# The shift of 32 layer norms computed on GpSimd instead of VectorE, in a Mamba block with a dense mixture of experts

## The chip, the cores and the metric

The kernel runs on one core of a Trainium2 chip. The metric is the device time of one execution in microseconds; lower is better. The core's engines each work through a queue of their own in order and wait for each other by semaphores: TensorE (PE in the profile; its weight loads are PEld), VectorE (DVE), ScalarE (ACT), GpSimd (POOL) and SyncE (SP, which only issues DMAs here).

## The reference

The input x has 16 sequences of 256 tokens, each token 128 numbers. All is float32. Cut to what matters:

```python
def block(x):                                    # the Mamba block
    x = x + mamba(layernorm(x, ln1_g, ln1_b))    # norm "a"
    h = layernorm(x, ln2_g, ln2_b)               # norm "b"
    return x + relu(h @ ffn_w1.T + ffn_b1) @ ffn_w2.T + ffn_b2

def experts(x):                                  # all 8 experts for every token
    return sum((silu(x @ Wg[e]) * (x @ Wu[e])) @ Wd[e] for e in range(8))

x = layernorm(x + block(x))                      # norm "c"
x = layernorm(x + experts(x))                    # norm "e"

# inside mamba, for each of 256 channels and 16 states, along the 256 tokens:
h = exp(dt * A) * h + dt * B * xc
y = sum over states of h * C;  y = (y + D * xc) * silu(z)
```

A layer norm is (x - mean) / sqrt(variance + 1e-5) over the 128 numbers of a token. Written as x * rs + nb, rs is the variance plus 1e-5 to the power -1/2, and nb = -mean * rs is the shift that this case is about.

## The kernel before, in words

The 4096 tokens go through in eight groups of 512. The tokens of a group lie on the 128 partitions in four columns of tokens, so each norm of a group has four means and four powers per partition: tiles of 128x4. Eight groups times the four norms a, b, c, e make 32 norms.

The work of a group is cut into stages, written as Python generators: `stage_a` (norm a, projections, convolution, and `dt`, ending with `u` = dt * xc on GpSimd, L369), the scan over 32 pairs of channel half and state, `stage_c` (output projection `po` L504, norm b, the two-layer network `pf` L549 and `pff` L539, norm c), the experts (`pg` L596, `pu` L605, `acc` L615, with the SiLU on ScalarE at L598 and the product on VectorE at L606), and `stage_e` (norm e and the store). The scan does four things for each of its 32 steps: the decay `dA` on ScalarE (L441), the injection `dBx` on GpSimd (L452), the recurrence and the product `hC` on VectorE (L460, L462), and the sum into `y`, which is on TensorE (L479) while there are no experts to run and on GpSimd (L481) otherwise. `yt` (L489, VectorE) multiplies the finished y by the gate, and `po` reads it.

The order of all instructions is written out by hand in strings of one-letter words: `PRE` before the first scan, `FILL` until the first group reaches its experts, `TURN` after that. A word advances one thing: `s` a scan step, `i` an injection, `d` a decay, `a` an addition into y, `u`, `x`, `w` the three parts of an expert slice, `m` a filler of four transposes on TensorE (L715), and a capital letter moves every running stage of a kind on to its next `yield`. So the place of a stage's instruction in its engine's queue is set by the number of `yield`s ahead of it, and each queue is then worked through in this order. The experts of one group run among the scan of the next.

A norm is in three parts. `norm_stats` takes statistics on VectorE (L244, L246), adds 1e-5 (`ve`, L248), and raises to -1/2 on GpSimd (`rs`, L250). Two `yield`s later `norm_shift` makes the shift on VectorE in one instruction (`nb`, L256: mean times -1 times rs). `norm_apply` then makes four instructions on ScalarE with rs as scale and nb as bias (L262). In `stage_c` two additions on GpSimd make the second residual: `res` = x1 + x (L516), issued right after the power of norm b, and `res` + bias (L520), issued after the shift.

Of the kernel before, what the change touches and what calls it, by code (L numbers as in the profile page):

```python
# [8 lines left out]
FP = mybir.dt.float32  # L9
AF = mybir.ActivationFunctionType  # L10
ALU = mybir.AluOpType

P = 128
# [8 lines left out]
NTT = TB // P  # L22
# [82 lines left out]
def kernel(  # L105
# [25 lines left out]
    nc = tc.nc  # L131
# [11 lines left out]
    small = ctx.enter_context(tc.tile_pool(name="small", bufs=4))  # L143
# [91 lines left out]
    def as4(t):  # L235
        return t.rearrange("p (c d) -> p c d", d=DM)

    def norm_stats(src, name):

        n = src.shape[1]  # L240
        st = small.tile([P, NTT, 6], FP, tag="st", name=f"st_{name}")
        mv = small.tile([P, NTT, 2], FP, tag="mv", name=f"mv_{name}")
        for c in range(n):
            nc.vector.bn_stats(st[:, c, :], src[:, c, :])  # L244
        for c in range(n):
            nc.vector.bn_aggr(mv[:, c, :], st[:, c, :])  # L246
        ve = small.tile([P, NTT], FP, tag="ve", name=f"ve_{name}")
        nc.vector.tensor_scalar(ve[:, :n], mv[:, :n, 1], EPS, None, ALU.add)  # L248
        rs = small.tile([P, NTT], FP, tag="rs", name=f"rs_{name}")
        nc.gpsimd.tensor_tensor(rs[:, :n], ve[:, :n], mhalf[:, :n], ALU.pow)  # L250
        return mv[:, :n, 0], rs[:, :n]

    def norm_shift(stats, name):
        mean, rs = stats
        nb = small.tile([P, NTT], FP, tag="nb", name=f"nb_{name}")[:, : mean.shape[1]]
        nc.vector.scalar_tensor_tensor(nb, mean, -1.0, rs, ALU.mult, ALU.mult)  # L256
        return rs, nb

    def norm_apply(src, dst, scale):
        rs, nb = scale  # L260
# [49 lines left out]
    def stage_a(g):  # L310
        xt = x_tiles[g]
        s = state[g] = {}
        yield
        stats = norm_stats(xt, f"a{g}")
        yield
        yield
        scale = norm_shift(stats, f"a{g}")
        yield
        xh = wide("xh", f"xh{g}", 2, W[g])
        norm_apply(xt, as4(xh), scale)  # L320
        yield
        pt = yield from take(f"pxn{g}", W[g])
        transpose(pt, as4(xh))
        yield
        xn = wide("xn", f"xn{g}", 2, W[g])
        nc.scalar.activation(xn, pt, AF.Identity, bias=b1_sb[:, 0:1], scale=g1_sb[:, 0:1])
        done(f"pxn{g}")
        yield
        s["conv"] = set()
        s["xc"] = wides("xc", f"xc{g}", 2, NH, W[g])  # L330
        for h in range(NH):
            conv = stage_conv(g, h, xn)
            next(conv)
            next(conv)
            running["B" if g == 1 else "A"].append(conv)
        if g < 2:
            running["G"].append(stage_gate(g, xn))
        while (NH - 1) not in s["conv"] or 0 not in s["conv"]:
            yield
            yield  # L340
        R = DTR + 2 * NS
        pd = yield from take(f"pd{g}", W[g])
        for h in range(NH):
            nc.tensor.matmul(
                pd[0:R, :], lhsT=xpw[:, h, :], rhs=s["xc"][:, h, :], start=(h == 0), stop=(h == NH - 1)
            )
        yield
        dbc = act.tile([R, TB], FP, tag="dbc", bufs=2, name=f"dbc{g}")[:, : W[g]]
        nc.scalar.copy(dbc, pd[0:R, :])  # L349
        done(f"pd{g}")  # L350
        bc = s["bc"] = dram.tile([2 * NS, TB], FP, tag="bc", name=f"bc{g}")[:, : W[g]]
        nc.scalar.dma_start(out=bc, in_=dbc[DTR:R, :])
        yield
        dt = s["dt"] = wides("dt", f"dt{g}", 2, NH, W[g])
        u = s["u"] = wides("u", f"u{g}", 2, NH, W[g])
        for h in range(NH):
            pv = yield from take(f"pv{g}_{h}", W[g])
            nc.tensor.matmul(pv, lhsT=dtw[:, bass.ts(h, P)], rhs=dbc[0:DTR, :], start=True, stop=True)
            yield
            nc.scalar.activation(dt[:, h, :], pv, AF.Identity, bias=dtb[:, h : h + 1])  # L360
            done(f"pv{g}_{h}")
            yield
        yield from silu_time()
        nc.scalar.activation(dt, dt, AF.Softplus)  # L364
        yield
        for h in range(NH):

            engine = nc.vector if g == 0 and h == 0 else nc.gpsimd
            engine.tensor_tensor(u[:, h, :], dt[:, h, :], s["xc"][:, h, :], ALU.mult)  # L369

            engine.memset(dt[:, h, :].rearrange("p (b l) -> p b l", l=L)[:, :, 0:1], FAR)
            if g > 0:
                yield
                yield
        s["ready"] = True
        if g > 1:
            yield from stage_gate(g, xn)
# [118 lines left out]
    def stage_c(g):  # L496
        s = state[g]
        xt = x_tiles[g]
        xtf = xt.rearrange("p c d -> p (c d)")
        yield  # L500
        po = yield from take(f"po{g}", W[g])
        for c in range(W[g] // P):
            for h in range(NH):
                nc.tensor.matmul(  # L504
                    po[:, bass.ts(c, P)], lhsT=s["yt"][:, h, bass.ts(c, P)], rhs=outw[:, h, :],
                    start=(h == 0), stop=(h == NH - 1),
                )
        yield
        yield
        x1 = wide("x1", f"x1{g}", 1, W[g])  # L510
        nc.vector.tensor_add(x1, po, xtf)
        done(f"po{g}")
        stats = norm_stats(as4(x1), f"b{g}")

        res = wide("res", f"res{g}", 1, W[g])
        nc.gpsimd.tensor_tensor(res, x1, xtf, ALU.add)  # L516
        yield
        yield
        scale = norm_shift(stats, f"b{g}")
        nc.gpsimd.tensor_tensor(  # L520
            as4(res), as4(res), fb2_bc[:, :].unsqueeze(1).to_broadcast([P, W[g] // P, DM]), ALU.add
        )
        yield
        xh = wide("xh", f"x1h{g}", 2, W[g])
        norm_apply(as4(x1), as4(xh), scale)
        yield
        pt = yield from take(f"ph{g}", W[g])
        transpose(pt, as4(xh))
        yield
        h2 = wide("h2", f"h2{g}", 1, W[g])  # L530
        nc.scalar.activation(h2, pt, AF.Identity, bias=b2_sb[:, 0:1], scale=g2_sb[:, 0:1])
        done(f"ph{g}")
        yield
        r = wides("r", f"r{g}", 1, NF, W[g])
        po = None

        def second(f, start, stop):
            for c in range(W[g] // P):
                nc.tensor.matmul(  # L539
                    po[:, bass.ts(c, P)], lhsT=r[:, f, bass.ts(c, P)], rhs=w2[:, f, :],  # L540
                    start=start and c == 0, stop=stop and c == W[g] // P - 1, skip_group_check=True,
                )


        if g == 0:
            po = yield from take(f"pff{g}", W[g])
        for f in range(NF):
            pf = yield from take(f"pf{g}_{f}", W[g])
            nc.tensor.matmul(pf, lhsT=w1[:, bass.ts(f, P)], rhs=h2, start=True, stop=True)  # L549
            if g == 0 and f > 0:  # L550
                second(f - 1, f == 1, False)
            yield
            nc.scalar.activation(r[:, f, :], pf, AF.Relu, bias=fb1_sb[:, f : f + 1])  # L553
            done(f"pf{g}_{f}")
            yield
        if g > 0:
            po = yield from take(f"pff{g}", W[g])
            for f in range(NF - 1):
                second(f, f == 0, False)
                if f == 1:  # L560
                    yield
                    yield
        second(NF - 1, False, True)
        yield
        yield
        nc.vector.tensor_add(res, po, res)
        done(f"pff{g}")
        stats = norm_stats(as4(res), f"c{g}")
        yield
        yield  # L570
        scale = norm_shift(stats, f"c{g}")
        yield
        x2 = blocks("x2", f"x2{g}", 2, W[g] // P)
        norm_apply(as4(res), x2, scale)
        yield
        pt = yield from take(f"px{g}", W[g])
        transpose(pt, x2)
        yield
        x2T = wide("x2T", f"x2T{g}", 2, W[g])
        nc.scalar.copy(x2T, pt)  # L580
        done(f"px{g}")
        state[g] = dict(x2=x2, x2T=x2T)
        slices.extend((g, n) for n in range(NJ[g]))
        yield
# [35 lines left out]
    def stage_e(g):  # L620
# [8 lines left out]
        x2 = s["x2"]  # L629
        nc.vector.tensor_add(x2, as4(pt), x2)  # L630
        done(f"pao{g}")
        stats = norm_stats(x2, f"e{g}")
        yield
        yield
        scale = norm_shift(stats, f"e{g}")
        yield
        norm_apply(x2, x2, scale)
        nc.scalar.dma_start(out=tokens(out, g), in_=x2)
# [92 lines left out]
    while at["w"] < sum(NJ) or any(running.values()):  # L731
# [4 lines left out]
        g, k = scans[min(at["a"], len(scans) - 1)]  # L736
# [56 lines left out]
```

## Time and profile before

| | |
|---|---|
| median of 3 runs | 953.29 us (953.23 to 954.67) |
| the profiled execution's own time | 953.88 us |
| its span, first to last instruction | 952.1 us |
| TensorE busy | 909.8 us, 96% |
| VectorE busy | 755.6 us, 79% |
| ScalarE busy | 672.8 us, 71% |
| GpSimd busy | 662.4 us, 70% |
| mean granted clock of TensorE | 0.981 |

The page has one execution. Its slices show each engine's busy share in tenths over 40 equal pieces of the span, and the TensorE clock that was granted. A line of the timeline has the start in us from the first instruction, the length, engine, line of the kernel, operation, output and inputs, shape and count, and in brackets how long the engine stood idle before it and for whom. A line of the groups has the count, the busy time in us, the mean of one in ns, and the idle time before them in us with what ended it. A line of a table by stretch has the stretch in us, its length, and then for each engine its busy time and number of instructions, the granted clock, and the DMA share and rate.

A busy TensorE is not TensorE at its peak: ends of matrix products are modelled. Where a step of TensorE is measured here, it is from start to start.

### The profile page before, as it was taken

To read this page: it belongs to the slowest core of one execution; us is meant where nothing else is said; L and a number is where in the kernel's file an instruction comes from. 1 tells how busy PE (TensorE), PEld (TensorE's weight loads), DVE (VectorE), ACT (ScalarE), POOL (GpSimd) and SP (SyncE) were. 2 spreads that over 40 slices of the span, in tenths; PEclk is the share of its full clock that TensorE was granted. 3 is DMA by queue.
4 is the path that set the end of the run, shared out by engine and by line. 5 is a ranking of instruction groups with operands and counts; after the bars stand their busy time and mean duration, and the time that the engine had idled before them with its cause. 6 is when DMAs were issued, how large, how long until landed. Compare 5 with 4: busy or idle time off the path is not lost. (4 is left out here: it accounts for less than half of the span.)

```text
span 952.1 us, 9052 instructions
## 1 busy us (share of the span) xinstructions
PE 909.8 (96%) x2528; PEld 421.0 (44%) x2528; DVE 755.6 (79%) x1179; ACT 672.8 (71%) x965; POOL 662.4 (70%) x558
## 2 busy tenths in 40 slices
PE   8898889989999999999999999999999999999996
PEld 4344534445344543445344544454344544454442
DVE  4599897988889888997989888987989799723222
ACT  5833387769788788779787879879888877432121
POOL 1586486987699678988698869988698799500000
PEclk9799899999999999999999999999999999999998
DMA  7788764545356345446346354645445454000000
GB/s 202 259 294 279 242 220 158 182 143 186 124 180 224 126 155 168 179 142 219 116 149 226 111 176 154 210 131 197 144 154 176 150 196 174 1 0 12 0 1 11
DMA packets 56258, 146.88 MB, mean 154 GB/s; under 512 B 7688, under 2 KB 20880, under 8 KB 56208
## 3 DMA queue, kind: packets, MB, share of 16 engines
q1 hardware_dynamic: 51600, 143.69, 44.5%
q10 hardware_dynamic: 4608, 2.62, 1.0%
q8 instruction: 20, 0.33, 0.1%
q14 instruction: 30, 0.25, 0.1%
HBM read 143.67 MB, written 2.62 MB: 154 GB/s over the span
## 5 line engine op out<-in xcount | busy, mean ns | idle before, releaser
L460 DVE TENSOR_TENSOR_SCAN dA<-dA,dBx 128x512 f32<-128x512 f32 x256 | 312.8, 1222 | 26.4 <-ACT dA L441 24.0
L452 POOL TENSOR_TENSOR dBx<-B,u 128x512 f32<-128x512 f32 x256 | 321.1, 1277 | 11.3 <-DMA B<-bc 7.3
L481 POOL TENSOR_TENSOR y<-y,hC 128x512 f32<-128x512 f32 x217 | 277.5, 1281 | 11.4 <-DVE hC L462 5.5
L615 PE MATMUL acc<-h,wd 128*128 128x512 f32 x512 | 255.8, 599 | 0.0
L606 DVE TENSOR_TENSOR h<-pu,h 128x512 f32<-128x512 f32 x256 | 172.4, 684 | 101.2 <-PE pu L605 99.9
L596 PE MATMUL pg<-x2T,wg 128*128 128x512 f32 x512 | 251.7, 598 | 0.3 <-DVE h L606 0.2
L605 PE MATMUL pu<-x2T,wu 128*128 128x512 f32 x512 | 245.3, 594 | 0.9 <-ACT h L598 0.9
L598 ACT ACTIVATE h<-pg 128x512 f32<-128x512 f32 x256 | 146.3, 597 | 124.3 <-PE pg L596 122.6
L441 ACT ACTIVATE dA<-dt,A 128x512 f32<-128x512 f32 x256 | 170.3, 684 | 81.6 <-DVE hC L462 77.4
L462 DVE TENSOR_TENSOR hC<-dA,C 128x512 f32<-128x512 f32 x256 | 176.9, 691 | 14.4
L596 PEld LDWEIGHTS pg<-x2T,wg 128*128 128x128 f32 x512 | 96.8, 192 | 125.9 <-issue 103.6
L605 PEld LDWEIGHTS pu<-x2T,wu 128*128 128x128 f32 x512 | 96.3, 191 | 122.1 <-issue 98.7
L615 PEld LDWEIGHTS acc<-h,wd 128*128 128x128 f32 x512 | 94.6, 191 | 113.4 <-issue 110.6
L250 POOL TENSOR_TENSOR rs_e<-ve_e,mhalf 128x4 f32<-128x4 f32 x8 | 8.1, 1017 | 139.7 <-DVE ve_e L248 139.7
L598 ACT ACT_TABLE_LOAD x78 | 100.1, 1283 | 1.4
L441 ACT ACT_TABLE_LOAD x74 | 94.9, 1283 | 1.7 <-ACT dbc L349 0.4
L479 PE MATMUL py<-hC,ident 128*128 128x512 f32 x78 | 44.2, 674 | 7.9 <-DVE hC L462 7.9
L369 POOL TENSOR_TENSOR u<-dt,xc 128x512 f32<-128x512 f32 x15 | 19.6, 1305 | 33.0 <-ACT dt L364 33.0
L410 DVE SCALAR_TENSOR_TENSOR hc<-pi,cw,hc 128x510 f32<-128x510 f32 (+2 forms) x48 | 35.5, 745 | 5.3 <-ACT hc L403 4.1
L715 PE MATMUL busy<-ident 128*128 128x128 f32 x204 | 35.7, 302 | 2.8 <-POOL mhalf L191 1.4
L715 PEld LDWEIGHTS busy<-ident 128*128 128x128 f32 x204 | 25.9, 154 | 24.1 <-issue 10.5
L553 ACT ACTIVATE r<-pf,fb 128x512 f32<-128x512 f32 x32 | 21.2, 687 | 18.5 <-PE pf L549 18.5
(83 smaller groups left out, 592.8 us busy)
## 6 DMA issues: line engine op xcount, KB each, us to landing
B<-bc SPq DMA_DIRECT2D x128, 512.0 KB, 4.7
C<-bc SPq DMA_DIRECT2D x128, 512.0 KB, 4.7
xt<-in_x_dram SPq DMA_DIRECT2D x8, 256.0 KB, 4.3
wg<-in_Wg_dram SPq DMA_DIRECT2D x8, 256.0 KB, 6.0
wu<-in_Wu_dram SPq DMA_DIRECT2D x8, 256.0 KB, 5.7
wd<-in_Wd_dram SPq DMA_DIRECT2D x8, 256.0 KB, 6.1
out_dram<-x ACTq DMA_DIRECT2D x8, 256.0 KB, 5.0
bc<-dbc ACTq DMA_DIRECT2D x8, 64.0 KB, 1.6
```

Source lines behind the costliest of these rows:

```text
L441: nc.scalar.activation(s["dA", k], s["dt"][:, h, :], AF.Exp, scale=A_sb[:, h, n : n + 1])
L452: nc.gpsimd.tensor_tensor(s["dBx", k], s["B", k // NC][:, k % NC, :], s["u"][:, k // NS, :], ALU.mult)
L460: nc.vector.tensor_tensor_scan(dA, dA, s.pop(("dBx", k)), 0.0, ALU.mult, ALU.add)
L462: nc.vector.tensor_mul(hC, dA, s["C", k // NC][:, k % NC, :])
L479: nc.tensor.matmul(s["py"], lhsT=ident, rhs=hC, start=first, stop=False)
L481: nc.gpsimd.tensor_tensor(y, y, hC, ALU.add)
L596: nc.tensor.matmul(pg[:, cols], lhsT=wg[:, e, bass.ts(f, P)], rhs=s["x2T"], start=True, stop=True)
L598: nc.scalar.activation(s["h", j], pg, AF.Silu)
L605: nc.tensor.matmul(pu[:, cols], lhsT=wu[:, e, bass.ts(f, P)], rhs=s["x2T"], start=True, stop=True)
L606: nc.vector.tensor_mul(s["h", j], pu, s["h", j])
L615: nc.tensor.matmul(s["acc"], lhsT=wd[:, e, f, :], rhs=h[:, cols], start=(e == 0 and f == 0), stop=(e == NE - 1 and f == NF - 1),)
L715: nc.tensor.transpose(t[:, bass.ts(c, P)], ident, ident)
```

## The change

The shift is made inside `norm_stats`, right behind the power. VectorE now makes `nm`, minus the mean, ahead of `ve`. GpSimd multiplies it by rs (`nb`) directly after the power. `norm_shift` and its place two `yield`s later go away; the number of `yield`s up to `norm_apply` stays the same. In `stage_c` the first residual addition moves behind the two `yield`s, to the second.

```diff
         for c in range(n):
             nc.vector.bn_aggr(mv[:, c, :], st[:, c, :])
+
+        nm = small.tile([P, NTT], FP, tag="nm", name=f"nm_{name}")
+        nc.vector.tensor_scalar(nm[:, :n], mv[:, :n, 0], -1.0, None, ALU.mult)
         ve = small.tile([P, NTT], FP, tag="ve", name=f"ve_{name}")
         nc.vector.tensor_scalar(ve[:, :n], mv[:, :n, 1], EPS, None, ALU.add)
         rs = small.tile([P, NTT], FP, tag="rs", name=f"rs_{name}")
         nc.gpsimd.tensor_tensor(rs[:, :n], ve[:, :n], mhalf[:, :n], ALU.pow)
-        return mv[:, :n, 0], rs[:, :n]
-
-    def norm_shift(stats, name):
-        mean, rs = stats
-        nb = small.tile([P, NTT], FP, tag="nb", name=f"nb_{name}")[:, : mean.shape[1]]
-        nc.vector.scalar_tensor_tensor(nb, mean, -1.0, rs, ALU.mult, ALU.mult)
-        return rs, nb
+        nb = small.tile([P, NTT], FP, tag="nb", name=f"nb_{name}")
+        nc.gpsimd.tensor_tensor(nb[:, :n], nm[:, :n], rs[:, :n], ALU.mult)
+        return rs[:, :n], nb[:, :n]
...
     # stage_a; stage_c's norm c and stage_e alike
-        stats = norm_stats(xt, f"a{g}")
-        yield
-        yield
-        scale = norm_shift(stats, f"a{g}")
+        scale = norm_stats(xt, f"a{g}")
+        yield
+        yield
         yield
...
     # stage_c, norm b
-        stats = norm_stats(as4(x1), f"b{g}")
+        scale = norm_stats(as4(x1), f"b{g}")
+        yield
+        yield
 
         res = wide("res", f"res{g}", 1, W[g])
         nc.gpsimd.tensor_tensor(res, x1, xtf, ALU.add)
-        yield
-        yield
-        scale = norm_shift(stats, f"b{g}")
         nc.gpsimd.tensor_tensor(
             as4(res), as4(res), fb2_bc[:, :].unsqueeze(1).to_broadcast([P, W[g] // P, DM]), ALU.add
         )
```

More of the change, by code (lines that the diff above doesn't have):

```diff
@@ L567, in stage_c @@
         done(f"pff{g}")
-        stats = norm_stats(as4(res), f"c{g}")
+        scale = norm_stats(as4(res), f"c{g}")
         yield
         yield
-        scale = norm_shift(stats, f"c{g}")
         yield
@@ L631, in stage_e @@
         done(f"pao{g}")
-        stats = norm_stats(x2, f"e{g}")
+        scale = norm_stats(x2, f"e{g}")
         yield
         yield
-        scale = norm_shift(stats, f"e{g}")
         yield
```

## The prediction

> **What bounds the kernel now.** The page's slices come first: which engine is full, and where.
>
> ```profile
> PE   8898889989999999999999999999999999999996
> ...
> PEclk9799899999999999999999999999999999999998
> ...
> PE 14%; DVE 1%; issue 0%; ACT 0%; POOLq 0%; DVEq 0%
> ```
>
> A slice is 24 us. From the tenth slice on TensorE is full; the other engines have gaps. The last line is the chain that ended last: 14% of the span TensorE, nearly nothing else. In order of time that chain runs on TensorE without a gap from 805.71 to 942.36, and only the last norm follows. So norm work counts only where TensorE waits for it, and the next view is the timeline around TensorE's waits. Between 277 and 800 there is one large wait per group of tokens, at L504, and it comes back every 105.3 us. One such group, followed back:
>
> ```profile
> 569.80 1.02 POOL L250 TENSOR_TENSOR rs_e<-ve_e,mhalf 128x4 f32<-128x4 f32 x1 [7.71 <-DVE ve_e L248]
> 570.79 1.28 POOL L452 TENSOR_TENSOR dBx<-B,u 128x512 f32<-128x512 f32 x1
> ...
> 585.00 1.27 POOL L369 TENSOR_TENSOR u<-dt,xc 128x512 f32<-128x512 f32 x1 [0.50 <-ACT dt L364]
> ...
> 621.83 2.49 POOL L481 TENSOR_TENSOR y<-y,hC 128x512 f32<-128x512 f32 x2
> ...
> 623.14 1.73 DVE L489 TENSOR_TENSOR yt<-y,zg 128x512 f32<-128x512 f32 x1 [0.42 <-POOL y L481]
> ...
> 624.93 1.27 PE L504 MATMUL po<-outw,yt 128*128 128x128 f32 x9 [1.74 <-DVE yt L489]
> ```
>
> TensorE stands 1.74 us for yt; yt on VectorE stands 0.42 us for GpSimd's y; GpSimd has run without a pause since u at 585.00, and u waited 0.50 us for ScalarE's dt. So the period closes through TensorE, then dt on ScalarE, then u to y on GpSimd, yt, TensorE. The norms' GpSimd work (rs_b, rs_a, rs_c, rs_e) lies before u, never between u and yt. The five u of this kind (269, 374, 480, 585, 690) each have 0.50 to 0.52 us of slack. That slack is what the change must fit into.
>
> The other place is the start of the first expert work, where the engines wait for each other in turn:
>
> ```profile
> 104.25 0.17 DVE L248 TENSOR_SCALAR ve_b<-mv_b 128x4 f32<-128x4 f32 x1
> 104.50 1.01 POOL L250 TENSOR_TENSOR rs_b<-ve_b,mhalf 128x4 f32<-128x4 f32 x1 [7.95 <-DVE ve_b L248]
> 105.47 1.26 POOL L516 TENSOR_TENSOR res<-x,xt 128x512 f32<-128x512 f32 x1
> 105.54 1.21 DVE L256 SCALAR_TENSOR_TENSOR nb_b<-mv_b,rs_b 128x4 f32<-128x4 f32 x1 [1.12 <-POOL rs_b L250]
> ...
> 106.79 1.65 ACT L262 ACTIVATE x1h<-x,nb_b,rs_b 128x128 f32<-128x128 f32 x4 [6.24 <-DVE nb_b L256]
> ...
> 107.34 1.63 PE L269 MATMUL ph<-ident,x1h 128*128 128x128 f32 x4 [3.74 <-ACT x1h L262]
> ```
>
> Here the shift nb_b is on the path: ScalarE and, through it, TensorE wait for it. Four numbers per partition took 1.21 us, because the residual addition on GpSimd started 0.07 us before it.
>
> **The change part by part.** The durations needed:
>
> ```profile
> L452 POOL TENSOR_TENSOR dBx<-B,u 128x512 f32<-128x512 f32 x256 | 321.1, 1277 | 11.3 <-DMA B<-bc 7.3 <-DVE dA L460 2.5 <-DVE hC L462 1.4
> ...
> L250 POOL TENSOR_TENSOR rs_b<-ve_b,mhalf 128x4 f32<-128x4 f32 x8 | 8.1, 1017 | 35.7 <-DVE ve_b L248 35.7
> ...
> L256 DVE SCALAR_TENSOR_TENSOR nb_b<-mv_b,rs_b 128x4 f32<-128x4 f32 x8 | 6.0, 746 | 2.3 <-POOL rs_b L250 2.3
> ...
> L371 POOL MEMSET dt<- 128x2 f32 x15 | 1.5, 102 | 0.9
> ...
> L248 DVE TENSOR_SCALAR ve_b<-mv_b 128x4 f32<-128x4 f32 x8 | 1.4, 170 | 0.3
> ```
>
> Removed: 32 nb on VectorE, 6.0 + 4.2 + 3.3 + 3.1 = 16.6 us busy for b, c, a, e, and 6.7 us of waiting for the power before them. In the full stage this buys nothing: VectorE already stands 2.67 us at 556.59 for TensorE's pu, 2.35 us at 588.87 for ScalarE's dA, 0.42 us at yt for GpSimd. It is early there, and gets earlier. ScalarE's applications of a, c and e are not waiting for nb either (545.56, 550.23 and 575.07 follow the instruction before them without a gap); x1h at 526.42 starts as its predecessor ends.
>
> Added on VectorE: 32 nm, the same instruction, shape and stride as ve (170 ns). Neither needs the other, and after a ve the next instruction starts 0.07 us later (523.86, then 523.93), so ve and the power move by 0.07 us.
>
> Added on GpSimd: 32 multiplications of 128x4, unseen in this trace; call the duration d. From below the MEMSET's 0.10, from above the power's 1.02 on the same tiles. The nearest row of the operation is the 128x512 multiplication, 1277 ns. The Trainium skill's GPSIMD Engine Reference, Performance versus the Vector engine, gives 4497 ns for a two-input add of 2048 elements; the line through both is 2.10 ns an element with 0.20 us fixed, so my estimate is d = 0.21 us. I take it over the power's row, since the power's microsecond for four elements against 1.28 for 512 products says that the power, not the launch, costs it. No price below zero: it is an extra instruction on a queue that waits in order.
>
> The nb waits for rs on its own engine. Such a wait costs about 0.08 us (res at 525.10 took 1.28 and its successor started at 526.45), while independent ones overlap by about 0.05. So everything behind it on GpSimd moves by 0.07 + 0.08 + d - 0.05 + 0.03 = 0.13 + d = 0.34 us (0.03 because after rs the next now starts 0.99 after its start, not 1.02). Queued behind are dBx, y and, after b, the two res additions, whose order with the rest stays as it was: no other GpSimd instruction stood between them. The waits at the next rs (0.72, 3.1, 7.7 us in the steady groups) take up the delays of b, a and c; that of e meets the 0.50 us at u and leaves 0.16. Scans have their dBx at least 1.1 us ahead in this stage (closest is the scan at 533.76, whose dBx ended at 532.6). Steady groups: 0. It would cost from d = 0.37 on. No DMA moves; the SyncE and TensorE orders are the same.
>
> The wait that is added is ScalarE's for nb on GpSimd, in place of VectorE's; dA and h are queued behind the application. In the steady groups it is met early: nb_e would be ready at 571.2 for an application at 575.07, nb_b at 525.5 for one at 526.42, nb_c at 543.8 for 545.56. It would cost from d of about 1.1 us in b, the tightest.
>
> On the path there are three places:
> - Start: rs_a 5.23 to 5.30, nb from 6.40 to 6.61, first application 6.65 instead of 6.49: +0.16.
> - First b norm: rs_b 104.57 to 105.58, nb 105.66 to 105.87, x1h 105.91 instead of 106.79: -0.88. VectorE no longer stands 1.12 us there nor is held by the addition, so its scan runs 2.1 us earlier and dA behind x1h is ready. TensorE goes from ph to pf in its own order (filler transposes between), so pf, r, pff, the c norm and the first experts follow by 0.88; nb_c is ready about 0.9 us before ScalarE reaches it. GpSimd's u of the second group waits 4.6 us for dt, so the gain passes on.
> - End: rs_e 945.94 to 946.01, nb 947.10 to 947.31, application 947.35 instead of 947.18: +0.17.
>
> Sum: 0.16 - 0.88 + 0.17 = -0.55 us, made against the profiled execution: 953.88 us, of which 952.1 is span. It stands 0.59 above the median of 953.29. Carried to the median: **952.7 us**.
>
> Two rules of the skill speak otherwise. First, the row: an nb on VectorE that nothing holds takes 163 ns, yet 591 is the median of b and 1225 the worst. The GPSIMD Engine Reference, Engine selection, says that a two-input elementwise operation belongs on VectorE and takes about twice as long on GpSimd. Twice 163 is d = 0.33: the three places lose 0.12 each, the sum is -0.19, 953.1 us, and u has 0.04 left. I keep 0.21, because the rule is for long tiles, but the change is no gift by it. Second, the clock. TensorE's gap before ph ends at 107.34 after 3.74 us, and the clock is at 0.50 from 107.6 to 114.4. TensorE: Matmul & The Clock Gate, The HAM clock gate, says that half rate follows an idle window of about 3.4 us. The gap shrinks to 2.86, so by the page the clock would stay: filler and pf at full rate bring the first pff from 114.2 to about 110.9, and the sum is near 3.3 - 0.33, or 950.3 us. But:
>
> ```profile
> 199.77:203.18 3.41, 1.13 (x10) 1.14 (x11) 2.92 (x3) 2.48 (x3) 3.28 (x3) 1.00 0.77 231
> 203.18:206.59 3.41, 3.41 (x10) 2.02 (x9) 3.31 (x13) 0.00 (x0) 0.00 (x0) 0.50 0.01 2
> ```
>
> The first number after the stretch is its length, then busy PE, PEld, DVE, ACT, POOL, then the clock. A gap of 2.63 us, with TensorE busy 1.13 of 3.41, halved the next stretch too. I keep the drop.
>
> **The rivals.**
> - The clock recovers (above), wholly or one stretch earlier: 950.0 to 951.4. For it: the shorter gap and earlier pf. Against: the 2.63 us gap. Chance 0.2.
> - The small multiplication costs what the power costs, d = 1.02, and GpSimd becomes the limit. Each of five u is late by 1.02 - 0.37 = 0.65 us, 3.25 in all; the three places lose 0.81 each, 2.43. -0.55 + 5.68 = +5.1: 958.4 us, slower. It decides from d = 0.62, where 3 x 0.41 + 5 x 0.25 - 0.55 passes 1.9 us. For it: the only 128x4 GpSimd row is 1.02. Against: 512 products take only 1.28. Chance 0.1.
> - The earlier events fall worse against the clock's stretches, between 134 and 145 where TensorE stands 1.4 us at pv and ran at half rate, so that more is slow: +2 to +3 us, 955.3 to 956.5. The runs shown spread by 1.4 us. Chance 0.08.
>
> **How the numbers follow.** The rest, 0.62, is the absorbed change, 951.5 to 954.3 by itself. 0.2% is 1.9 us, about what a measurement of this kernel tells from no change: faster is below 951.4, slower above 955.2. The range of 950.0 to 956.5 takes in the clock cases and leaves out the costly multiplication. Faster 0.2, within it 0.62, slower 0.18.
>
> **What would show it.** Right: nb on GpSimd near 0.2 us; u in the steady groups still waiting for dt, with about 0.16 us instead of 0.50; the period still 105.3; x1h near 105.9; VectorE idle longer at pu. Wrong: no idle time left before u and a longer wait at L504; a clock row other than 0.50 after 107.6; or nb held by a VectorE instruction.

## The result and the profile after

Over 22 runs each the changed kernel has a median of 954.65 us (952.97 to 957.34), the kernel before 953.61 us (952.16 to 954.67). The ratio is 1.0013, interval 1.0007 to 1.0018: about 1 us slower, where 0.55 us faster was forecast. In a second set of runs it came to 954.46 us against 953.39, ratio 1.0009, interval 1.0001 to 1.0017. The profiled execution of the changed kernel happens to be its longest, 957.34 us, with a span of 955.5. A second one (the twelfth run below) has a span of 951.3; the text says where the two differ.

The page of the changed kernel: the slices of TensorE, of its clock, and the shares of the chain that ended last.

```profile
PE   8898899989999999999999999999999999999996
...
PEclk8799989999999999999999999999999999999998
...
PE 14%; DVE 1%; issue 0%; ACT 0%; POOL 0%; POOLq 0%; DVEq 0%
```

Nothing in it tells of a change. TensorE is as full as before to within a tenth, and among the lines of the chain that the page lists the norm's shift does not appear. The reading has to go to the places that the prediction named. The timeline around one steady group of the changed kernel, GpSimd, VectorE and TensorE together:

```profile
571.05 1.02 POOL L253 TENSOR_TENSOR rs_e<-ve_e,mhalf 128x4 f32<-128x4 f32 x1 [7.45 <-DVE ve_e L251]
572.15 0.20 POOL L255 TENSOR_TENSOR nb_e<-nm_e,rs_e 128x4 f32<-128x4 f32 x1
572.30 1.27 POOL L450 TENSOR_TENSOR dBx<-B,u 128x512 f32<-128x512 f32 x1
...
583.48 2.50 POOL L479 TENSOR_TENSOR y<-y,hC 128x512 f32<-128x512 f32 x2
...
585.43 1.09 DVE L487 TENSOR_TENSOR yt<-y,zg 128x512 f32<-128x512 f32 x1
...
586.18 1.47 POOL L367 TENSOR_TENSOR u<-dt,xc 128x512 f32<-128x512 f32 x1 [0.20 <-ACT dt L362]
...
624.52 1.74 DVE L487 TENSOR_TENSOR yt<-y,zg 128x512 f32<-128x512 f32 x1 [0.63 <-POOL y L479]
...
626.31 0.38 PE L502 MATMUL po<-outw,yt 128*128 128x128 f32 x1 [1.95 <-DVE yt L487]
```

And the two lines of the kernel before that answer to the fourth and fifth of these, which the prediction did not look at:

```profile
582.00 2.50 POOL L481 TENSOR_TENSOR y<-y,hC 128x512 f32<-128x512 f32 x2
...
584.43 0.68 DVE L489 TENSOR_TENSOR yt<-y,zg 128x512 f32<-128x512 f32 x1
```

The small multiplication takes 0.20 us and starts 0.08 after the power, as forecast. u still waits for dt, now 0.20 us instead of 0.50. But u itself takes 1.47 us instead of 1.27, and the product yt of the first half, in front of it on VectorE, takes 1.09 instead of 0.68. The order of events shows why. Before, the last y ended at 584.50 (582.00 + 2.50) and yt started at 584.43, so that yt ran in GpSimd's pause. After, yt starts at 585.43 while y runs until 585.98, and it ends 0.54 us after that. u starts at 586.18 beside it and ends 0.20 late. From u to the last y GpSimd has no pause, so yt of the second half waits 0.63 us instead of 0.42, and TensorE waits 1.95 us at po instead of 1.74.

At the first b norm the forecast came out, on GpSimd, ScalarE and TensorE:

```profile
104.44 1.01 POOL L253 TENSOR_TENSOR rs_b<-ve_b,mhalf 128x4 f32<-128x4 f32 x1 [7.44 <-DVE ve_b L251]
105.53 0.20 POOL L255 TENSOR_TENSOR nb_b<-nm_b,rs_b 128x4 f32<-128x4 f32 x1
105.68 1.27 POOL L516 TENSOR_TENSOR res<-x,xt 128x512 f32<-128x512 f32 x1
...
105.76 1.65 ACT L261 ACTIVATE x1h<-x,nb_b,rs_b 128x128 f32<-128x128 f32 x4 [5.34 <-POOL nb_b L255]
...
106.31 0.71 PE L268 MATMUL ph<-ident,x1h 128*128 128x128 f32 x2 [2.84 <-ACT x1h L261]
```

The groups give the same over all norms:

```profile
L367 POOL TENSOR_TENSOR u<-dt,xc 128x512 f32<-128x512 f32 x15 | 20.6, 1372 | 30.9 <-ACT dt L362 30.9
...
L487 DVE TENSOR_TENSOR yt<-y,zg 128x512 f32<-128x512 f32 x13 | 17.7, 1361 | 4.6 <-POOL y L479 4.6
...
L255 POOL TENSOR_TENSOR nb_b<-nm_b,rs_b 128x4 f32<-128x4 f32 x8 | 1.6, 202 | 0.6
...
L249 DVE TENSOR_SCALAR nm_b<-mv_b 128x4 f32<-128x4 f32 x8 | 1.4, 170 | 0.3
```

A mean of 1372 ns (it was 1305) for an instruction that takes 1270 when nothing holds it is the first hint that something beside it does. The period between steady groups is 105.42 us without a clock drop; it was 105.31.

### The profile page after: what moved, and what is told of

It reads as the page before. It is cut to its first block, busy times and chain, and to the rows that moved or that the text cites. A ratio compares the mean times of both kernels' runs of the same rounds, so it can differ in the third digit from the quotient of the medians.

```text
span 955.5 us, 9100 instructions
## 1 busy us (share of the span) xinstructions
PE 912.2 (95%) x2528; PEld 423.1 (44%) x2528; DVE 746.2 (78%) x1179; ACT 672.1 (70%) x965; POOL 669.0 (70%) x590
## 5 line engine op out<-in xcount | busy, mean ns | idle before, releaser
L367 POOL TENSOR_TENSOR u<-dt,xc 128x512 f32<-128x512 f32 x15 | 20.6, 1372 | 30.9 <-ACT dt L362 30.9
L253 POOL TENSOR_TENSOR rs_b<-ve_b,mhalf 128x4 f32<-128x4 f32 x8 | 8.1, 1017 | 37.7 <-DVE ve_b L251 37.7
```

## The experiments

Periods below are from po to po, or from u to u, in periods without a half-rate stretch.

**1 and 2: one norm alone.** A choice by name puts the shift on GpSimd for one norm only.

```diff
+        if name[0] == "b":            # second kernel: "e"
+            nb = small.tile([P, NTT], FP, tag="nb", name=f"nb_{name}")
+            nc.gpsimd.tensor_tensor(nb[:, :n], nm[:, :n], rs[:, :n], ALU.mult)
...
     # norm b only: the first residual addition behind the two yields, as in the change
```

> The kernel before, with the shift of norm b alone on GpSimd behind the power (all groups; its residual addition behind the two yields); norms a, c, e as before. Theory (yt of the first half, held between GpSimd's last y and u, is what the change costs per group, and only the delay from norm e reaches it): x1h near 105.8 instead of 106.8; u of the later groups waits 0.50 us as before, yt of the first half stays at 0.68 us, period 105.3; time 0.5 to 0.9 us under before, 952.7 to 953.1. Rival 1 (the first expert work comes earlier, but the clock's half-rate stretches between 107 and 145 take all of it back): 953.6, no difference, with the half-rate time between 100 and 150 us still near 13.7 us. Rival 2 (every 0.34 us on GpSimd counts, whichever norm it comes from): period above 105.4.

> The kernel before, with the shift of norm e alone on GpSimd. Theory: no gain at the first b norm; in each of the five steady groups yt of the first half takes 1.09 instead of 0.68 us, u 1.47 instead of 1.27, period 105.42 instead of 105.31, wait of TensorE at po about 0.2 us longer; with 0.17 at the end of the run 0.6 to 0.8 us above before, and more where the clock falls in the longer po wait: 954.2 to 955.5. Rival (the 0.34 us is absorbed by the 0.50 us before u, and after's loss has to do with the clock after the first experts alone): period 105.3, 953.8.

Norm b alone: 952.75 us, ratio 0.9989, interval 0.9982 to 0.9995. Faster, as the theory had it, with yt at 0.68 and u waiting 0.49 to 0.54. One thing neither side expected: the period is 105.19, 0.12 under before. The steady b norms were on the path after all. The kernel before, VectorE then ScalarE:

```profile
525.80 0.59 DVE L256 SCALAR_TENSOR_TENSOR nb_b<-mv_b,rs_b 128x4 f32<-128x4 f32 x1
...
526.42 0.49 ACT L262 ACTIVATE x1h<-x,nb_b,rs_b 128x128 f32<-128x128 f32 x1
```

With norm b's shift on GpSimd, GpSimd then ScalarE:

```profile
524.26 0.20 POOL L256 TENSOR_TENSOR nb_b<-nm_b,rs_b 128x4 f32<-128x4 f32 x1
...
525.36 0.48 ACT L271 ACTIVATE x1h<-x,nb_b,rs_b 128x128 f32<-128x128 f32 x1
```

Before, nb_b ended at 526.39 and x1h started 0.03 later. The instruction ahead of it on ScalarE had ended at 526.42 too (525.12 + 1.30), so x1h looked as if it only followed. In a row without a wait, ScalarE's instructions overlap by 0.06: in the second fence the predecessor ends at 525.41 (524.11 + 1.30) and x1h starts at 525.36. That 0.06 was a hidden wait for nb_b. Without it the four transposes ph behind x1h take 1.08 us instead of 1.15, and from there to u all stands 0.07 to 0.09 us nearer to po. The rest of the 0.12 lies between u and the next po and is not traced.

Norm e alone: 955.46 us, ratio 1.0018, interval 1.0009 to 1.0028. The mechanism is the theory's, on VectorE and GpSimd:

```profile
585.76 1.10 DVE L498 TENSOR_TENSOR yt<-y,zg 128x512 f32<-128x512 f32 x1
...
586.51 1.50 POOL L378 TENSOR_TENSOR u<-dt,xc 128x512 f32<-128x512 f32 x1 [0.19 <-ACT dt L373]
```

The period is 105.44 to 105.48, a little more than expected. The gain of b and the loss of e, -0.9 and +1.8 us, add to about the change's +1.0.

**3: the change without norm e.**

```diff
+        if name[0] != "e":            # a, b, c as in the change; e: shift on VectorE, two yields later
             nb = small.tile([P, NTT], FP, tag="nb", name=f"nb_{name}")
             nc.gpsimd.tensor_tensor(nb[:, :n], nm[:, :n], rs[:, :n], ALU.mult)
```

> The changed kernel with the shift of norm e back on VectorE two yields later, as before; a, b, c on GpSimd. Theory: the first b norm's gain stays (x1h 105.8), yt of the first half back at 0.68 us, u waits 0.50 us, period 105.31, no half-rate stretch at the po waits: 0.6 to 1.2 us under after, 953.0 to 953.6. Rival 1 (the clock after the first experts eats the gain): with after, 954.3 to 954.7. Rival 2 (the delays of a, b, c add up at u as well): u waits under 0.3 us.

953.32 us, ratio 0.9994, interval 0.9986 to 1.0002: 1.3 us under the change, at the kernel before. u waits 0.50 to 0.55 us in all five groups, so the 0.3 us that a, b and c add on GpSimd do not reach it. The period is 105.17 to 105.20. That is norm b's period, yet the time stands 0.6 us above the run with b alone; the two intervals overlap, and this difference is not explained. Against the expectation the last steady wait at po was 2.05 us instead of 1.73, with a half-rate stretch behind it. The trace shows the same collision by another way, on VectorE and GpSimd:

```profile
686.18 0.69 DVE L471 TENSOR_TENSOR hC<-dA,C 128x512 f32<-128x512 f32 x1 [0.46 <-POOL y L490]
...
687.38 0.68 DVE L498 TENSOR_TENSOR yt<-y,zg 128x512 f32<-128x512 f32 x1
...
687.60 1.59 POOL L378 TENSOR_TENSOR u<-dt,xc 128x512 f32<-128x512 f32 x1 [0.52 <-ACT dt L373]
```

VectorE stood 0.46 us for GpSimd's y two instructions ahead of yt, yt came only 0.22 us ahead of u (0.57 in the group before), and u took 1.59.

**4: the other half of yt.**

```diff
-            nc.vector.tensor_mul(s["yt"][:, h, :], y, s["zg"][:, h, :])
+            engine = nc.gpsimd if h == NH - 1 and name not in owner else nc.vector
+            engine.tensor_tensor(s["yt"][:, h, :], y, s["zg"][:, h, :], ALU.mult)
```

> The kernel before, with yt of the second half (the product that TensorE's po waits for, 1.73 us on VectorE although it takes 0.69 alone, since GpSimd's next y runs beside it) on GpSimd right behind the last y, for the groups whose y lies in SBUF. If yt on VectorE is held by GpSimd's instruction beside it (both inputs in SBUF), the product takes about 1.27 us on GpSimd with no wait, po starts about 0.5 us earlier in six groups and GpSimd's later work moves by 0.9 us, taken up before the next power (7.7 us): period 104.8, 950 to 951.5. If yt's 1.73 us is its own work and not contention, GpSimd takes as long or longer and the time is 953.6 or above.

950.79 us, ratio 0.9968, interval 0.9957 to 0.998, period 104.79. On GpSimd the product takes 1.26 us, with po on TensorE behind it:

```profile
620.10 1.26 POOL L490 TENSOR_TENSOR yt<-y,zg 128x512 f32<-128x512 f32 x1
...
621.41 0.38 PE L505 MATMUL po<-outw,yt 128*128 128x128 f32 x1 [1.33 <-POOL yt L490]
```

In the last group of the kernel before, where no y follows on GpSimd, the same product takes 0.69 us on VectorE too:

```profile
820.68 0.69 DVE L489 TENSOR_TENSOR yt<-y,zg 128x512 f32<-128x512 f32 x1 [0.26 <-POOL y L481]
```

So the 1.73 us of yt on VectorE were 0.69 of work and 1.04 of being held by the y that runs beside it on GpSimd.

**5: the delay without the change.**

```diff
+        if name[0] == "e":
+            for i in range(2):
+                dm = small.tile([P, NTT], FP, tag=f"dm{i}", name=f"dm{i}_{name}")
+                nc.gpsimd.tensor_tensor(dm[:, :n], ve[:, :n], mhalf[:, :n], ALU.mult)
```

> The kernel before, all shifts on VectorE as before, and two added 128x4 multiplications on GpSimd behind the power of each norm e, whose results nobody reads: the delay without the change. Theory (any 0.3 us on GpSimd between the power of norm e and u does it, through yt of the first half): delay 0.30 us, yt of the first half 1.0 to 1.1 instead of 0.68 us, u 1.43 to 1.47 instead of 1.27, period 105.40 to 105.42, 0.4 to 1.2 us above before. Rival (the shift's own dependence, or VectorE without its shift, is what costs): period 105.31, u waits 0.2 us and takes 1.27, time as before.

958.18 us, ratio 1.0048, interval 1.0035 to 1.006: far more than expected, at the same 0.30 us of delay. yt stays at 0.68, u takes 1.40, the period is 105.51 to 105.59. The theory had one place; here there are two. On GpSimd and VectorE:

```profile
571.55 0.36 POOL L254 TENSOR_TENSOR dm_e<-ve_e,mhalf 128x4 f32<-128x4 f32 x2
...
574.84 0.75 DVE L260 SCALAR_TENSOR_TENSOR nb_e<-mv_e,rs_e 128x4 f32<-128x4 f32 x1
```

and the same instruction on VectorE in the kernel before:

```profile
574.08 0.46 DVE L256 SCALAR_TENSOR_TENSOR nb_e<-mv_e,rs_e 128x4 f32<-128x4 f32 x1
```

The shift that stays on VectorE also has two inputs in SBUF, and is now held 0.29 us longer. VectorE and ScalarE behind it are late: dt ends 15.26 us after the start of the power instead of 15.12. Since VectorE is late as well, yt starts only when y ends and is not held, but it stands beside u. Two effects, 0.10 at po and 0.14 at dt, make the 0.2 to 0.3 us of period. The rest of the loss, in the profiled execution, is a half-rate stretch at 626.56 (1.6 us) and 1.6 us in the last group, where yt of the first half takes 1.83. So the delay costs without the change as well, and moving the shift away even spares something.

**6: yt with one input.**

```diff
+            if h == 0 and g > 1:
+                nc.vector.tensor_scalar(s["yt"][:, h, :], y, D_sb[:, h : h + 1], None, ALU.mult)
+            else:
                 nc.vector.tensor_mul(s["yt"][:, h, :], y, s["zg"][:, h, :])
```

> The changed kernel, with yt of the first half (groups 2 to 7) made of y alone, times a number per partition, in place of y times the gate: one SBUF input instead of two; it leaves out the gate of that half. Theory (yt and u are lengthened because VectorE's two SBUF inputs and GpSimd exclude each other): yt of the first half no longer waits for GpSimd's y, u takes 1.27 us with about 0.15 to 0.2 us of wait left, period back at 105.31, 0.4 to 1.2 us under after: 953.5 to 954.2. Rival (u is longer because of something else that runs beside it, the delay itself sets the period): u 1.47, period 105.42, time as after, 954.7.

```profile
582.43 0.82 DVE L488 TENSOR_SCALAR yt<-y,D 128x512 f32<-128x512 f32 x1
...
583.16 1.27 POOL L367 TENSOR_TENSOR u<-dt,xc 128x512 f32<-128x512 f32 x1 [0.20 <-ACT dt L362]
```

VectorE's yt and GpSimd's u, in the changed kernel with one input of yt gone. The delay is all there, u waits only 0.20 us, and u takes 1.27. Against the theory yt is not free: the last y holds this form too. But it ends 0.28 us after that y instead of 0.54, so it meets u for 0.08 us instead of 0.34. (In the last group, where it stands longer beside GpSimd's dBx, dBx takes 1.47.) So the run shows that yt has to be out of u's way, not that the second input alone is what bars it. The period falls to 105.17, 0.25 under the change and not the 0.1 expected, since b's steady gain of 0.12 is no longer covered. The time is 951.82 us, below the 953.5 to 954.2 expected, ratio to before 0.9985, interval 0.9978 to 0.9992; five periods make 1.25 of the 2.8 us to the changed kernel. This is the run that says what the delay costs the period: nothing (105.17, as without norm e's shift in run 3), once yt is out of u's way.

**7 to 10: without the collisions.** Run 7 combines the shift of the first b norm on GpSimd with the fourth run's yt; run 8 puts u of the first half on VectorE besides; run 9 has b's shift on GpSimd for all groups, both halves of yt on GpSimd, and that u; run 10 is run 9 with all four shifts on GpSimd.

```diff
-            engine = nc.vector if g == 0 and h == 0 else nc.gpsimd
+            engine = nc.vector if h == 0 and g != 1 else nc.gpsimd      # u: runs 8, 9, 10
...
+            engine = nc.vector if name in owner else nc.gpsimd          # yt: runs 9, 10
```

> A version meant to beat both: the kernel before, with the shift on GpSimd for the first b norm alone (-0.9 us in norm-b-only, against before), and yt of the second half on GpSimd (-2.8 us in that run). If both gains add: 949.9 to 950.4. If the clock after the first experts falls worse with both: 951 to 952.

> The version with the first b norm's shift and yt of the second half on GpSimd, and besides u of the first half on VectorE (groups 2 to 7), which has a pause of 2.3 us behind it: GpSimd is rid of 1.37 us and of its wait for dt in each group. If GpSimd's chain from u to the last y sets the period: y ends up to 1 us earlier, period 104.0 to 104.5, 947 to 949. If u on VectorE (two SBUF inputs) is held by GpSimd's instructions and holds them in turn, or TensorE has no more wait to lose: period 104.8, 950 or above.

> Norm b's shift on GpSimd in all groups (a, c, e on VectorE), both halves of yt on GpSimd behind their last y (where y lies in SBUF), u of the first half on VectorE (groups 2 to 7): no VectorE instruction with two SBUF inputs is left beside GpSimd there but u. In the run with yt of the first half still on VectorE, it took 1.82 us beside GpSimd and TensorE stood 0.64 us at pg behind it. If that hold is what costs: pg's 0.64 us goes in five groups and 1 us in the last, period 104.2 to 104.5, 943.5 to 945.5. If GpSimd's added 1.2 us meets the last y instead: 947 to 949.

> As the kernel just named, but with the shift of all four norms on GpSimd, as in the changed kernel. Theory (norm e's delay costs only where yt of the first half and u meet): with both out of the way the period is the same as in that kernel within 0.03 us, and the time differs by start and end alone, 0.2 to 0.4 us above it. Rival (the 0.3 us of norm e costs on GpSimd's chain itself, whatever stands on VectorE): period 0.15 to 0.2 longer, 1 to 1.5 us above it.

Run 7: 948.86 us, ratio 0.9957, interval 0.9943 to 0.997. That is below the expected range, but in ratio just the two gains together (0.9989 times 0.9968). Run 8: 947.9 us, ratio 0.9941, interval 0.9929 to 0.9954, within its expected range, but with periods of 104.90 to 105.04, not 104.0 to 104.5. yt of the first half, now 1.82 us beside GpSimd in four groups, makes TensorE wait 0.64 at pg (start to start, beyond the usual step of 0.43). Run 9: **944.61 us**, ratio 0.991, interval 0.9897 to 0.9924, period 104.64 (104.2 to 104.5 expected). It beats both kernels.

Run 10: 946.8 us, ratio 0.9929, interval 0.9917 to 0.9941, period 104.91. The theory said 0.03 us of period, the rival 0.15 to 0.2, and 0.27 were measured. As I had put it, for yt and u alone, the theory failed. The reason lies in u on VectorE, first in run 10, then in run 9:

```profile
584.99 0.96 DVE L367 TENSOR_TENSOR u<-dt,xc 128x512 f32<-128x512 f32 x1
```

```profile
583.32 0.68 DVE L378 TENSOR_TENSOR u<-dt,xc 128x512 f32<-128x512 f32 x1
```

Another VectorE instruction with two SBUF inputs. It starts 71.1 us behind po in both, ends 0.28 us later in run 10, where it lies otherwise against GpSimd's y, and the next po comes 0.27 later. So, as the traces have it (no run tests this u alone), the delay costs wherever such an instruction comes to lie beside GpSimd's on the path, not at yt alone.

**11 and 12: the clock.** The eleventh run is the fourth with norm e's shift on GpSimd, the twelfth the changed kernel again.

> The kernel with yt of the second half on GpSimd (950.79 us, period 104.80), with the shift of norm e alone on GpSimd besides. Norm e alone cost 1.8 us against before: five periods longer by 0.15 to 0.17 and the end by 0.17 give 1.0, the rest would be half-rate stretches of 3.41 us (1.6 us each) after TensorE's wait at po of 2.2 instead of 2.0 us. Here that wait is 1.75 us at most. If the rest is the clock behind a longer wait: 951.7 to 952.0, period 104.96, no half-rate stretch after po. If it is something else that comes with norm e: 952.4 to 952.8.

> The changed kernel once more, for a second profiled execution of it (the first was the slowest of its 22). Theory: period 105.42, wait at po 2.2 us start to start; between none and two half-rate stretches behind the five po waits, and each costs 1.6 us; time 954.2 to 955.0. If the first execution's two stretches were no part of the usual course, none here, and the time is then explained by periods, start and end alone: 953.6 to 954.0.

Run 11: 951.14 us, ratio 0.9974, interval 0.9964 to 0.9984, period 105.00, no half-rate stretch behind the steady waits at po. Against its own base, run 4, norm e costs some 0.4 to 0.6 us (0.8 between the profiled spans), less than even the 1.0 expected and far from 1.8. Run 12: 954.46 us; its profiled execution (span 951.3) has the period of 105.45 and none of the two drops of the first. It also lacks the drop behind the first wait at po, near 202, that the other execution and the kernel before have. The table by stretch shows when they come. First the changed kernel's first execution:

```profile
305.17:308.58 3.41, 1.53 (x6) 0.74 (x5) 2.81 (x4) 3.33 (x5) 3.33 (x4) 1.00 0.53 164
308.58:311.99 3.41, 3.41 (x15) 3.20 (x16) 2.51 (x4) 0.81 (x1) 0.91 (x1) 0.50 0.40 117
728.41:731.83 3.42, 1.45 (x6) 0.64 (x4) 2.74 (x4) 3.34 (x5) 3.34 (x4) 1.00 0.66 237
731.83:735.24 3.41, 3.41 (x15) 3.38 (x16) 2.43 (x4) 0.82 (x1) 1.00 (x1) 0.50 0.03 11
```

then its second, and the kernel before at its emptiest stretch of a steady wait at po:

```profile
725.68:729.09 3.41, 1.49 (x5) 0.58 (x4) 2.76 (x4) 3.33 (x5) 3.33 (x4) 1.00 0.64 219
```

```profile
411.39:414.80 3.41, 1.64 (x9) 0.97 (x8) 2.96 (x4) 3.33 (x5) 3.33 (x3) 1.00 0.57 192
```

The clock changes on a fixed grid of 3.41 us. Take, for every wait at po from the second group on, in all fourteen profiles, the emptiest stretch of the grid. With up to 1.45 us of TensorE busy the next stretch ran at half rate every time (10 of 10), from 1.59 on it never did, and between 1.49 and 1.57 it went both ways (3 drops in 7). The kernel before has 1.64 to 2.01 in its five steady groups. With 0.2 us more of waiting the changed kernel comes to about 1.45 to 1.5 where the wait lies wholly in one stretch, and stays higher where two stretches share it. Its first execution had 1.45 and 1.53 and dropped both times; its second had 1.49 once and did not drop, which is within the band where it went both ways. Such a drop makes its period 107.0 us, 1.6 more. The Trainium skill (TensorE: Matmul & The Clock Gate, The HAM clock gate) speaks of an idle window of about 3.4 us; the length agrees, but here windows with TensorE over 40% busy (1.45 of 3.41) were idle enough, and the measurement decides.

## Why the prediction was wrong

**d and the waits of nb: right.** d was forecast as 0.21 us and is 0.203; twice the free shift of VectorE would have been 0.33. The delay on GpSimd, 0.34 forecast, shows as 0.3: u's wait fell from 0.50 to 0.20 (0.16 forecast). In the steady groups the applications of a, c and e do not wait for nb, as said.

**"Meets the 0.50 us at u and leaves 0.16. Steady groups: 0": the step that failed.** The slack was read rightly from the line of u, and the delay fits in it. But slack in time is not all there is: the pause before u was in use. VectorE's yt of the first half stood just there, and it and GpSimd's instructions exclude each other: yt grew from 0.68 to 1.09 us and u from 1.27 to 1.47, and where yt is done sooner (run 6) u is back at 1.27. The Trainium skill has the rule, in SBUF — State Buffer, Who interferes with whom: a VectorE instruction with two inputs in SBUF contends with a GpSimd instruction that reads SBUF. The traces agree: in the kernel before, the recurrence and hC, whose dA lies in PSUM, stand beside GpSimd's instructions 241 and 220 times and take 1.21 to 1.23 and 0.69 us, as they do alone, while nb_e, with both inputs in SBUF, takes 0.45 to 0.47 beside them and 0.15 to 0.16 alone. That run 6's form with one input was held as well, this rule does not say. The prediction used exactly this at nb_b (1.21 us beside the residual addition) and saw yt at 1.73 in its own fence without asking why, when the other half takes 0.68. Measured, norm e costs 0.15 us of period by itself and 0.23 on top of b; by itself it cost 1.8 us of time, of which the clock's share is not shown.

**The same term has a gain that was missed.** "x1h at 526.42 starts as its predecessor ends" was read as no wait; it was 0.06 late, and b's shift gains 0.12 a period. Steady groups are not 0 but -0.12 + 0.23 = +0.11.

**First b norm, -0.88: right at x1h, smaller behind it.** x1h moved from 106.79 to 105.76, 0.9 once the start of the two executions is set equal (a u of the start, at 44.97 and 44.84). u of the next group moved only from 159.84 to 159.11, which is 0.6 set equal in the same way. In between lies the clock, in the kernel before:

```profile
107.60:114.43 6.83, 6.72 (x18) 3.74 (x18) 6.69 (x10) 2.91 (x6) 2.94 (x3) 0.50 0.50 169
138.32:145.15 6.83, 6.83 (x9) 2.35 (x8) 6.50 (x8) 3.00 (x5) 6.75 (x6) 0.50 1.01 362
```

and in the changed kernel:

```profile
107.19:110.60 3.41, 3.35 (x11) 2.20 (x12) 3.34 (x5) 1.57 (x3) 3.41 (x3) 0.50 0.57 202
134.50:144.74 10.24, 10.24 (x12) 3.15 (x11) 7.89 (x9) 4.45 (x6) 10.16 (x9) 0.50 0.92 302
```

One stretch less at half rate, as the rival "the clock recovers" had it, and the first experts start 2.4 us earlier; then one stretch more, as the rival "fall worse between 134 and 145" had it. Both came true and cancel: 13.65 us at half rate either way, in all fourteen profiles. The five with the first b norm's shift on VectorE have 6.83 and 6.83, eight of the nine with it on GpSimd have 3.41 and 10.24, and run 9 has 6.83 and 6.83 although its shift is on GpSimd, so the pattern is not fixed by the shift alone. That the two go together was not foreseen. From the u near 45 to the u near 159 those five take 114.73 us on average, the six others that leave u on GpSimd 114.29: about half of the 0.88 came through. The half rate at 107 itself stayed for one stretch, as the prediction kept it against the skill's rule.

**Start and end.** At the end nb_e starts 1.09 us behind the start of its power and takes 0.20, as forecast. At the start the first application moved from 6.49 to 6.62, by 0.13 of the 0.16 forecast; whether anything later moves with it cannot be told from the executions' own spread (that u lies between 44.1 and 45.2 in the kernels run here).

**The sum, for the first execution** (spans 952.1 and 955.5, +3.45): -0.73 up to u of the second group, +0.03 to the third, four periods +0.44 and the half-rate stretch in one of them +1.56, and +2.15 from there on: a half-rate stretch of 1.6, and about 0.6 for the longer wait, a wait of 0.62 instead of 0.34 us at pg near 809 (start to start, beyond the usual step), and the last norm. Without the two stretches it would be +0.3. The second execution is 0.8 shorter than the kernel before, but only because it lacks the drop near 202, worth 1.6; without that it would be +0.8. The median stands at +1.0, so the usual run may have some part of a half-rate loss: the mean granted clock is 0.980 over the changed kernel's 36 runs and 0.982 over the 83 of before that ran beside the experiments, and one stretch in 955 us is 0.0018. Runs of equal clock don't settle it (at 0.981 the means are 954.5 and 954.2, at 0.982 953.5 and 953.5, at 0.980 954.8 and 953.1), and in runs without a profile the stretches can't be seen. So the longer period behind norm e is shown, and the clock's share of the 1.0 stays open.

**"GpSimd becomes the limit", d = 1.02: fell,** since d is 0.20. Its picture of five late u was right, for another reason.

## What to carry to other kernels

Before slack is spent, look at what else uses it: an idle stretch of GpSimd may be the place in which VectorE's instruction with two SBUF inputs runs unhindered. A row whose length differs from its twin's (yt 0.68 and 1.73, u 1.27 and 1.47) says that something may hold it, and on the path that was worth more here than the idle times: taking such rows apart went with most of the 8.8 us of run 9, while the change itself lost 1. And "no idle time before it" is no proof of no wait where neighbours normally overlap.

## What the runs showed of the hardware

The clock's threshold behind a wait at po is sharp in these records, near 1.5 us of TensorE busy in 3.41, so that 0.2 us more of a wait of 2 us can bring a drop. It is no general threshold. In the kernel before, the first half-rate stretch of the pair from 138 to 145 shown above follows this one:

```profile
134.91:138.32 3.41, 2.02 (x5) 0.59 (x4) 3.31 (x5) 2.88 (x5) 3.41 (x4) 1.00 0.83 274
```

Six of the profiles have such a drop there after 2.02 or 2.03 us of busy TensorE. What else counts is open.

Where VectorE and GpSimd exclude each other and start nearly together, either may get through first. In the last group of the kernel before, VectorE, then GpSimd:

```profile
788.82 0.68 DVE L489 TENSOR_TENSOR yt<-y,zg 128x512 f32<-128x512 f32 x1
...
788.85 1.79 POOL L452 TENSOR_TENSOR dBx<-B,u 128x512 f32<-128x512 f32 x1
```

and in the run with norm b alone:

```profile
787.53 1.82 DVE L498 TENSOR_TENSOR yt<-y,zg 128x512 f32<-128x512 f32 x1
...
787.54 1.27 POOL L461 TENSOR_TENSOR dBx<-B,u 128x512 f32<-128x512 f32 x1
```

Here yt finishes at once or 1.14 us later, and TensorE's work behind it is about 1.0 us later by 805, as much as the whole change cost. In the fourteen profiles yt and GpSimd's dBx start within 0.03 us of each other twelve times. Nine times yt took 1.81 to 1.83 us and three times 0.68, and the recorded starts do not sort them: yt was held with a lead of 0.020 us and went through with one of 0.008. The profile of the kernel before is one of the three. Whether it falls the same way in every execution of one kernel is open; each was profiled once, the change twice.
